# A two-layer block on one core: how the slots' weights are turned, where W_out is loaded, and who normalises the last two groups

## The chip, the cores and the metric

The kernel runs on one core of one Trainium2 chip, as a single program. Its time is device microseconds of one execution, from the first instruction to the last with what lies around them; three executions are timed, and their median is the figure. One further execution is recorded by the hardware profiler and gives the profile.

The core has five engines that run in parallel, each through its own instructions in a fixed order: TensorE (PE, matrix products and 128 x 128 transposes against an identity), VectorE (DVE), ScalarE (ACT), GpSimd (POOL) and SyncE (SP, which here only issues DMAs). PEld is PE's loading of the stationary operand.

## The reference

The input x has 32 sequences of 512 tokens with 256 features, all in float32. Two layers are added to it, each after a layer norm without weights:

```python
x = x + attn(_layernorm(x), ...)
x = x + ffn(_layernorm(x), ...)

def attn(x):      # causal, one head
    q = tanh(x @ W_charge.T + b_charge)[..., 0]
    phi_c = mags * q[..., None] ** arange(5)
    shell = x @ W_shell.T + b_shell;  shell = shell / norm(shell)
    proj = shell @ omega.T + rff_bias
    phi = outer(phi_c, concat[cos(proj), sin(proj)]) @ W_combine.T
    attn = softmax(causal(phi @ phi.T * T / temp))
    return (attn @ (x @ W_v.T + b_v)) @ W_out.T + b_out

def ffn(x):       # 64 slots, each token takes its best 8
    h = gelu(concat[x, slot_mean] @ w1.T + b1)
    alpha = softmax over the top 8 of (h @ w2.T + b2) / (|tau| + 0.1), else 0
    gi = einsum('bts,btd->bsd', alpha, x) / (alpha.sum(1) + 1e-8)
    h_new = GRU(gi, slots)
    slot_values = h_new @ wv.T + bv
    return einsum('bts,bsd->btd', alpha, slot_values) @ wo.T + bo
```

`alpha` is needed with tokens on the partitions for the sum into the slots, and with slots on the partitions (turned) for the product that gives the slots' values back to the tokens.

## The kernel before

**Tiles and groups.** Two sequences make a group; there are 16 groups. A tile is 128 tokens x 256 features, so a group has 8 tiles. Each group goes through `features` (stages tokens, angles, phi), `attention` (weights, values), `router` (normal, router) and `slots` (taken, gru, given). The main tiles are named after their group: `xT` (x turned), `pf` and `sv` (the product of x with the folded weights `wf`, in PSUM and in SBUF), `phi`, `pl`, `pr`, `po` (logits, weights and output of attention; tile group 3 is the last row of 128 tokens, `pl_0` covers tokens 0 and 1), `xm` (the normalised x of the second layer), `xmT` (it, turned), `ph` (hidden layer), `prr`, `prt`, `rl` (router logits), `al` (alpha, L1510), `psi` (sum into the slots, L1534), `gi`, `prz`, `pn`, `rz`, `nn`, `rh`, `hn` (GRU), `alT` (alpha turned, L1655 and L1662), `pv`, `val` (slots' values) and `py` (what is given back, L1692; DVE adds it to x at L1706 and SP stores it).

**Who turns what.** PE turns a 128 x 128 block through PSUM (name `pt...`), and another engine copies it out. For x (from group 2 on) and xm (but in the last two groups, `LAST_BY_TENSOR = 2`) another way is used: a DMA writes the tile to memory (`xd`), four DMAs read it back so that each 32 x 32 block lies where it will have to be (`xmb`, `xb`), and DVE's transpose, which works block by block, does the rest (`xT`, L929; `xmT`, L881).

**The order.** Nothing runs in the order of the source. Each step is added to a plan with its engine, a cost, the steps that it follows and the buffers that it uses (`add`). `Plan.order` then places the steps one at a time: on each engine the ready step that could start first, ties by rank. A rank is made of the step's earliest time in its group (weighted with `LATE` against its latest), the group's number times `STRIDE`, and two numbers of its stage in `DELAY`, the second for the last groups. `HOP` is the plan's cost of going from one engine to another, `SWITCH` a penalty for changing PE's shape. So a change of these numbers changes the order of every engine's instructions, SP's DMAs included, and each engine then goes through its list in order and waits where an operand is missing. In the program each DMA issued by SP or ACT also waits for the landing of the eighth one before it.

**The start.** SP loads W_v, x_0 and x_1, small weights, x_2, the rest of the weights; ACT's queue loads W_charge, W_shell, W_out and two biases. DVE centres W_v (L432 to L435), PE multiplies it with W_out (`pw`, L446) into `wf`, which the first `pf` needs. The last setup steps on PE are `pt_hs` and `pgh` (L763, of the GRU's weights whh).

Of the kernel before, what the change touches and what calls it, by code (L numbers as in the profile page):

```python
# [23 lines left out]
SQ = 32  # L24
BY_TENSOR = 2
LAST_BY_TENSOR = 2
# [31 lines left out]
    "xT": 3,  # L58
    "xmT": 2,
    "xd": 2,  # L60
    "sv": 2,
    "xm": 2,
    "al": 2,
# [8 lines left out]
}  # L72


HOP = 0.23
TABLE = 1.28
SWITCH = 2.05
STRIDE = 33.83
LATE = 0.0

DELAY = {
    "setup": (0.0, 0.0),
    "load": (-30.3, -13.9),
    "tokens": (2.1, -9.2),
    "angles": (-45.8, -2.6),
    "phi": (5.7, -20.1),
    "weights": (-1.3, -2.7),
    "values": (18.9, -12.8),
    "normal": (16.1, 19.2),
    "router": (1.5, -3.5),  # L90
    "taken": (-8.0, -7.1),
    "gru": (26.3, -22.0),
    "given": (43.2, -16.5),
}

SPARE = 3
# [22 lines left out]
class Plan:  # L119
# [126 lines left out]
def block_kernel(ctx: ExitStack, tc: tile.TileContext, a: dict, out: bass.AP):  # L246
    nc = tc.nc
    x = a["x"]
    B = x.shape[0]
    NG = B // GB  # L250
# [7 lines left out]
    def lazy(tag, name, shape, dtype=F32):  # L258

        if tag not in pools:  # L260
            space = {"ps": bass.MemoryType.PSUM, "xd": bass.MemoryType.DRAM}.get(tag)
# [78 lines left out]
    ident = const("ident", [P, P])  # L340
# [20 lines left out]
    hs = const("hs", [P, D])  # L361
# [51 lines left out]
    def value_and_out(wv_ap, bv_ap, wo_t_ap, bo_ap, w_dst, b_dst, n, centred, engs, rank):  # L413

        at = 2 * n
        wv = part(at, 0, [P, KD, D])
        wo_t = part(at, KD * D, [P, KD, D])
        bv_rep = part(at, 2 * KD * D, [P, KD, P])
        bo = part(at, 2 * KD * D + KD * P, [P, D])
        of = wv.of  # L420
        bv = const(f"bv{n}", [P, KD])
        mean = const(f"wv_mean{n}", [P, KD])
        land = 3.5 if centred else None
        l_wv = load(engs[0], wv, rows(wv_ap), 256, rank=rank, land=land)
        l_wo = load(engs[1], wo_t, rows(wo_t_ap), 256, rank=rank, land=land)
        l_bv = load(engs[2], bv, bv_ap.rearrange("(k p) -> p k", p=P), 8, rank=rank)
        l_bo = load(engs[2], bo, bo_ap.partition_broadcast(P), 128, rank=rank)
        last = l_wv
        if centred:

            def centre():
                nc.vector.tensor_reduce(mean, wv(), AX.X, ALU.add)  # L432
                nc.vector.tensor_scalar(mean, mean, 1.0 / D, None, ALU.mult)
                for k in range(KD):
                    nc.vector.tensor_scalar(  # L435
                        wv()[:, k, :], wv()[:, k, :], mean[:, k : k + 1], None, ALU.subtract
                    )

            last = add("DVE", 1.6, centre, [l_wv], of, rank=rank)
        done, made = [], []  # L440
        for m in range(KD):
            pw = bank(f"pw{n}_{m}")

            def project(m=m, pw=pw):
                for k in range(KD):
                    nc.tensor.matmul(  # L446
                        pw()[:, 0:D],
                        wv()[:, k, m * P : (m + 1) * P],
                        wo_t()[:, k, :],
                        start=(k == 0),  # L450
                        stop=(k == KD - 1),
                    )
# [13 lines left out]

        def spread():
            for k in range(KD):
                nc.vector.tensor_scalar(
                    bv_rep()[:, k, :], onesP, bv[:, k : k + 1], None, ALU.mult  # L470
                )

        s = add("DVE", 0.5, spread, [l_bv, s_ones], of, rank=rank)
        pb = bank(f"pb{n}")

        def project_bias():
            for k in range(KD):
# [19 lines left out]
        return done, made  # L497
# [7 lines left out]
        bias_f[:, C_V:NF],  # L505
        0,
        True,
        ("SP", "ACT", "POOL"),
        -40.0,
    )  # L510
    l_bsh = [
# [15 lines left out]
    s = add("PE", 0.8, mean_shell, l_sh + [s_ones] + s_wv_pe, [pm], rank=-38.0)  # L527
# [5 lines left out]
    for q in range(P // SQ):  # L533
        for k in range(KD):
# [9 lines left out]
                    land=4.0,  # L544
# [7 lines left out]
    for bb in range(GB):  # L552
        r = slice(bb * SHELL, (bb + 1) * SHELL)
        for h in range(2):
# [15 lines left out]
                land=5.0,  # L570
# [146 lines left out]
    s = add("PE", 0.3, hs_transposed, [s_hs, s_ident], [pt_hs], rank=41.0)  # L717
# [16 lines left out]
    s = add("PE", 0.8, mean_hidden, [s_hst, l_w1s], [pb1] + w1s.of, rank=42.0)  # L734
# [612 lines left out]
    def router(g, s_x, ln):  # L1347

        xt = xs[g]
# [33 lines left out]
        def deviations():  # L1383
# [3 lines left out]
            nc.gpsimd.tensor_tensor(nmr, nm, rs, ALU.mult)  # L1387

        s_ln = add("POOL", 2.25, deviations, s_sq, [ln])
        s_xm = [  # L1390
            add(
                "ACT",
                0.51,
                lambda t=t: nc.scalar.activation(  # L1394
                    xm()[:, t, 0:D],
                    xt()[:, t, :],
                    AF.Identity,
                    bias=ln()[:, 4, t // NT, t % NT : t % NT + 1],
                    scale=ln()[:, 1, t // NT, t % NT : t % NT + 1],
                ),  # L1400
                [s_ln, s_one],
                [xm, xt, ln],
            )
# [96 lines left out]
        def sums():  # L1500
# [4 lines left out]
        s = add("DVE", 1.53, sums, [s], [rl, rest, asum])  # L1505
        s_al = [
            add(
                "POOL",
                1.1,
                lambda: nc.gpsimd.tensor_tensor(  # L1510
                    al().rearrange("p c b s -> p (c b) s"),
                    rl(),
                    asum().unsqueeze(2).to_broadcast([P, GT, SLOTS]),
# [8 lines left out]
    def slots(g, xm, al, s_al):  # L1522
# [48 lines left out]

        gi_t, s = halves("gi", gi, s_gi)
        plan.stage = "gru"

        rz = lazy("row", f"rz_{g}", [P, 2 * D])
        nn = lazy("half", f"nn_{g}", [P, D])
# [5 lines left out]
        def gates(dst, lo, n):  # L1582
# [42 lines left out]
            [rz, rh],  # L1625
        )
        s = add(
            "POOL",
            0.73,
            lambda: nc.gpsimd.tensor_tensor(nn(), nn(), rh(), ALU.add),  # L1630
            [s, s_n],
            [nn, rh],
        )
        s_nn = add("ACT", 0.42, lambda: nc.scalar.activation(nn(), nn(), AF.Tanh), [s], [nn], "exp")
        s = add(
            "POOL",
            0.73,
            lambda: nc.gpsimd.tensor_tensor(rh(), hs, nn(), ALU.subtract),
            [s_nn],
            [rh, nn],  # L1640
        )
# [5 lines left out]
        s = add("DVE", 0.94, new_state, [s], [rz, rh, nn, hn])  # L1647

        plan.stage = "given"
        pta = bank(f"pta_{g}")  # L1650
        al_t = lazy("row", f"alT_{g}", [P, T])

        def weights_turned():
            for c in range(NT):
                nc.tensor.transpose(  # L1655
                    pta()[:, c * P : (c + 1) * P],
                    al()[:, c, :, :].rearrange("p b s -> p (b s)"),
                    ident,
                )

        s_pta = add("PE", 0.58, weights_turned, s_al, [al, pta, al_t])
        s_alt = add("ACT", 0.54, lambda: nc.scalar.copy(al_t(), pta()), [s_pta], [pta, al_t])  # L1662

# [133 lines left out]
```

## Time and profile before

| | |
|---|---|
| timed runs | 699.04, 699.42, 700.35 us; median 699.42 |
| profiled execution | 698.51 us, its span 696.7 |
| PE busy | 665.6 us (96%) |
| DVE busy | 569.4 us (82%) |
| ACT busy | 461.5 us (66%) |
| POOL busy | 208.6 us (30%) |
| 128 x 128 transposes of `al` on PE (L1655) | 64, 273 ns each |
| copies of them out on ACT (L1662) | 16, 566 ns each |
| DMA | 83.26 MB, mean 120 GB/s |

The span runs from the first instruction to the last. A busy time is the union of an engine's instructions. Matmuls overlap, so that four transposes of 273 ns take less than their sum: the distance from one step's start to the next one's start is what PE really spends. A float32 matmul of the source appears as two records. In a line of the waits, the first name waits and the one after the arrow ended the wait; then total, times and the longest.

### The profile page before, as it was taken

The page shows a single profiled execution, that of the slowest core. Times are in us where ns is not written, and L with a number is a line of the kernel's source. Part 1 is how long each engine was busy: PE and PEld are TensorE (multiplying, and loading weights), DVE is VectorE, ACT ScalarE, POOL GpSimd, SP SyncE. Part 2 cuts the span into 40 slices and gives each one's busy share as a digit, 9 for nine tenths or more (in the row PEclk, how much of TensorE's full clock was granted, in tenths as well). Part 3 has the DMA queues.
Part 4 walks back from the last instruction along what each step waited for, and adds up shares of the span by engine and source line. Part 5 has one row for each costly group of instructions (what it writes and reads, how often), then busy time and mean ns, then how long its engine had stood idle before and what let it go on. Part 6 is the DMA issues. An engine that isn't in the chain of part 4 may idle for free.

```text
span 696.7 us, 12314 instructions
## 1 busy us (share of the span) xinstructions
PE 665.6 (96%) x3946; PEld 457.3 (66%) x3946; DVE 569.4 (82%) x1790; ACT 461.5 (66%) x1081; POOL 208.6 (30%) x406
## 2 busy tenths in 40 slices
PE   3979999999999999999999999999999999999975
PEld 3747766767666676766676676767667666667533
DVE  3979779789796988989798898979798896966554
ACT  1437777767766676775867677677677667778840
POOL 3640333124252232313333132323322224211120
PEclk9989999999999999999999999999999999999999
DMA  6683351552633735363544446263542611400203
GB/s 179 166 232 97 126 117 62 122 181 62 190 97 78 217 86 182 83 199 82 149 125 122 152 110 194 62 179 94 152 149 63 213 30 56 127 1 32 90 1 121
DMA packets 174256, 83.26 MB, mean 120 GB/s; under 512 B 123664, under 2 KB 173392, under 8 KB 174192
## 3 DMA queue, kind: packets, MB, share of 16 engines
q1 hardware_dynamic: 172880, 81.95, 42.2%
q8 instruction: 31, 0.51, 0.3%
q10 hardware_dynamic: 1104, 0.36, 0.2%
q14 instruction: 33, 0.27, 0.1%
q0 software_dynamic: 208, 0.17, 0.1%
HBM read 50.67 MB, written 31.46 MB: 118 GB/s over the span
## 4 chain that ended last, share of the span: by engine, by line
PE 83%; DVE 5%; ACT 4%; DMA 3%; SPq 2%; issue 1%; POOL 1%; DVEq 0%; POOLq 0%; ACTq 0%
PE po L1305 20%; PE pf L959 16%; PE ph L1422 8%; PE ptp L1299 5%; PE pl L1221 5%; PE pph L1164 5%; PE psi L1534 4%; PE py L1692 4%; PE prz L1584 3%; DMA x<-in_x_dram 2%; SPq L280 2%; PE prr L1445 2%; PE pv L1672 2%; PE pn L1584 2%; PE pp L1106 1%; ACT xm L1394 1%
## 5 line engine op out<-in xcount | busy, mean ns | idle before, releaser
L1305 PE MATMUL po<-sv,prT 128*128 128x256 f32 x640 | 150.5, 379 | 0.0
L959 PE MATMUL pf<-wfb,xT 128*128 128x321 f32 x448 | 129.0, 438 | 0.0
L1305 PEld LDWEIGHTS po<-sv,prT 128*128 128x128 f32 x640 | 116.5, 189 | 16.7 <-issue 1.1
L959 PEld LDWEIGHTS pf<-wfb,xT 128*128 128x128 f32 x448 | 82.3, 189 | 37.4 <-issue 3.9
L1262 ACT ACTIVATE pr<-lg,nm 128x128 f32<-128x128 f32 (+3 forms) x128 | 70.3, 550 | 15.4 <-DVE nm L1250 15.0
L1334 DVE SCALAR_TENSOR_TENSOR x<-po,den,x 128x256 f32<-128x256 f32 x128 | 58.0, 478 | 24.3 <-PE po L1305 23.1
L1394 ACT ACTIVATE xm<-x,lnb 128x256 f32<-128x256 f32 x128 | 66.3, 590 | 10.1 <-POOL lnb L1387 10.1
L1371 ACT ACTIVATE xm<-x,lnb 128x256 f32<-128x256 f32 x128 | 63.6, 501 | 5.9 <-POOL lnb L1359 5.8
L972 DVE SCALAR_TENSOR_TENSOR sv<-pf,lna,bias_f 128x321 f32<-128x321 f32 x128 | 62.7, 540 | 3.2 <-PE pf L959 2.6
L1510 POOL TENSOR_TENSOR al<-rl,asum 128x512 f32<-128x512 f32 x16 | 16.7, 1043 | 143.6 <-DVE asum L1503 142.0
L1250 DVE CUSTOM_DVE_ANT_0 lg<-pl,mask 128x128 f32<-128x128 f32 (+3 forms) x128 | 55.8, 480 | 3.2 <-PE pl L1221 2.8
L1317 ACT COPY prT<-ptp 128x384 f32<-128x384 f32 (+1 forms) x96 | 46.6, 511 | 13.8 <-PE ptp L1299 13.5
L1422 PE MATMUL ph<-xmT,w1b 128*128 128x512 f32 x112 | 52.5, 596 | 0.0
L1706 DVE TENSOR_TENSOR x<-py,x 128x512 f32<-128x512 f32 x64 | 40.0, 683 | 14.0 <-PE py L1692 14.0
L1359 POOL TENSOR_SCALAR lnb<-lnb 128x2 f32<-128x2 f32 (+1 forms) x48 | 12.1, 253 | 128.3 <-DVE x L1334 128.1
L1299 PE MATMUL ptp<-ident,pr 128*128 128x128 f32 x320 | 48.3, 276 | 1.0 <-ACT pr L1262 0.9
L800 DVE BATCH_NORM_STATS2 bna<-x 128x6 f32<-128x256 f32 x128 | 47.1, 414 | 0.0
L1299 PEld LDWEIGHTS ptp<-ident,pr 128*128 128x128 f32 x320 | 37.3, 140 | 13.7 <-issue 6.3
L1221 PE MATMUL pl<-phi 64*128 64x256 f32 (+1 forms) x384 | 45.3, 361 | 0.0
L1221 PEld LDWEIGHTS pl<-phi 64*128 64x128 f32 x384 | 31.2, 186 | 15.5 <-issue 7.6
L1152 DVE TENSOR_TENSOR tp<-tp,qs 128x1024 f32<-128x1024 f32 x32 | 39.2, 1225 | 2.2 <-ACT tp L1138 1.7
L1164 PE MATMUL pph<-tp,wc 64*64 64x256 f32 x640 | 38.2, 381 | 0.0
(169 smaller groups left out, 1252.5 us busy)
## 6 DMA issues: line engine op xcount, KB each, us to landing
x<-in_x_dram SPq DMA_DIRECT2D x32, 512.0 KB, 5.0
out_dram<-x SPq DMA_DIRECT2D x64, 256.0 KB, 2.5
xb<-in_x_dram SPq DMA_DIRECT2D x112, 128.0 KB, 2.7
xd<-xm SPq DMA_DIRECT2D x28, 512.0 KB, 4.4
xmb<-xd SPq DMA_DIRECT2D x112, 128.0 KB, 2.7
setup<-in_gru_whh_t_dram SPq DMA_DIRECT2D x1, 768.0 KB, 6.5
wih<-in_gru_wih_t_dram SPq DMA_DIRECT2D x1, 768.0 KB, 9.8
wfb<-wf SPq DMA_DIRECT2D x8, 40.1 KB, 3.4
```

The lines of the kernel that those rows point to most:

```text
L959: nc.tensor.matmul(pf()[:, 0:NF], tile_()[:, k, c * P : (c + 1) * P], w[:, k, :], start=(k == 0), stop=(k == KD - 1),)
L972: lambda t=t, pf=pf: nc.vector.scalar_tensor_tensor(sv()[:, t, :], pf()[:, 0:NF], ln()[:, 1, t : t + 1], bias_f, ALU.mult, ALU.add,),
L1164: nc.tensor.matmul(phs[h]()[bb * COMB : (bb + 1) * COMB, 0:HT], wc[r, m, :], tp()[r, m, bb * HT : (bb + 1) * HT], start=(m == 0), stop=(m ...
L1221: nc.tensor.matmul(pls[bb]()[:, off[i] + lo : off[i] + lo + w], phi()[r, 0, q : q + P], phi()[r, 1, k : k + w], start=True, stop=True,)
L1250: nc.vector.tensor_tensor_reduce(out=lg()[:, c], in0=pls[bb]()[:, c], in1=mask[:, T - w : T], scale=1.0, scalar=TOP, op0=ALU.add, op1=ALU.min,
L1262: nc.scalar.activation(pr()[:, c], lg()[:, c], AF.Exp, bias=nm(), scale=-1.0, accum_out=den()[:, tiles.index(i), bb : bb + 1],)
L1299: nc.tensor.transpose(pt()[:, j : j + P], prs[bb]()[:, j : j + P], ident)
L1305: nc.tensor.matmul(po()[:, d * D : (d + 1) * D], pr_t()[:, lo : lo + P], sv()[:, bb * NT + j, C_V:NF], start=(j == 0), stop=(j == i),)
L1334: nc.vector.scalar_tensor_tensor(xt()[:, t, :], po()[:, d * D : (d + 1) * D], den()[:, d, bb : bb + 1], xt()[:, t, :], ALU.mult, ALU.add, ...
L1371: lambda bb=bb, i=i: nc.scalar.activation(xm()[:, bb * NT + i, 0:D], xt()[:, bb * NT + i, :], AF.Square, bias=ln()[:, 2, bb, i : i + 1], a ...
L1394: lambda t=t: nc.scalar.activation(xm()[:, t, 0:D], xt()[:, t, :], AF.Identity, bias=ln()[:, 4, t // NT, t % NT : t % NT + 1], scale=ln()[ ...
L1422: nc.tensor.matmul(ph(), w1[:, k, :], dst()[:, k, :], start=(k == 0), stop=(k == KD - 1))
```

## The change

It does five things.

1. *The slots' weights.* In groups 0 to 13 `al` is written to memory by one DMA (`ad`, 256 KB), read back by four (`ab`, 64 KB each, in runs of 32 floats) and turned block by block by one DVE transpose into `alT`. The four PE transposes and ACT's copy stay in groups 14 and 15 only.
2. *W_out* is issued by SP after W_v and before the tokens, and no longer by ACT.
3. *xm of the last two groups* is made by DVE with a multiply and an add per token tile, in place of ACT's Identity with scale and bias.
4. *POOL's steps of the last two groups*: `al`, and two sums of the GRU (`nn`, `rh`), go to DVE.
5. *Ranks.* `HOP`, `SWITCH`, `STRIDE`, `LATE` and all of `DELAY` have new values, so that every engine's order is a new one. In a middle group the attention's tile groups now go 3, 2, 0 in place of 0, 2, 3, and the slots' `py` of group g stands among the logits of group g + 3.

```diff
-HOP = 0.23
+HOP = 0.44
 TABLE = 1.28
-SWITCH = 2.05
-STRIDE = 33.83
-LATE = 0.0
+SWITCH = 0.0
+STRIDE = 21.62
+LATE = 0.74

 DELAY = {
...
-    "load": (-30.3, -13.9),
-    "tokens": (2.1, -9.2),
...
-    "given": (43.2, -16.5),
+    "load": (-12.3, 2.7),
+    "tokens": (6.7, -6.0),
...
+    "given": (4.5, 5.6),
 }
...
-    ("SP", "ACT", "POOL"),
+    ("SP", "SP", "POOL"),
...
+        by_vector = g >= NG - LAST_BY_TENSOR
+
+        def moved(t):
+            b, c = divmod(t, NT)
+            bias, scale = ln()[:, 4, b, c : c + 1], ln()[:, 1, b, c : c + 1]
+            if by_vector:
+                nc.vector.tensor_scalar(
+                    xm()[:, t, 0:D], xt()[:, t, :], scale, bias, ALU.mult, ALU.add
+                )
+            else:
+                nc.scalar.activation(
+                    xm()[:, t, 0:D], xt()[:, t, :], AF.Identity, bias=bias, scale=scale
+                )
...
-                "POOL",
-                1.1,
-                lambda: nc.gpsimd.tensor_tensor(
+                "DVE" if by_vector else "POOL",
+                0.7 if by_vector else 1.1,
+                lambda: (nc.vector if by_vector else nc.gpsimd).tensor_tensor(
                     al().rearrange("p c b s -> p (c b) s"),
...
+        by_vector = g >= NG - LAST_BY_TENSOR
+        side, cost = ("DVE", 0.42) if by_vector else ("POOL", 0.73)
+        ev = nc.vector if by_vector else nc.gpsimd
...
-            lambda: nc.gpsimd.tensor_tensor(nn(), nn(), rh(), ALU.add),
+            lambda: ev.tensor_tensor(nn(), nn(), rh(), ALU.add),
...
-            lambda: nc.gpsimd.tensor_tensor(rh(), hs, nn(), ALU.subtract),
+            lambda: ev.tensor_tensor(rh(), hs, nn(), ALU.subtract),
...
+        if g >= NG - LAST_BY_TENSOR:
...
+        else:
+            ad = lazy("ad", f"ad_{g}", [T, P])
+            ab = lazy("row", f"ab_{g}", [P, T // SQ, SQ])
+            s_a = add("SP", 0.7,
+                lambda: nc.sync.dma_start(
+                    out=ad().rearrange("(c p) s -> p c s", p=P),
+                    in_=al().rearrange("p c b s -> p c (b s)"),
+                ), s_al, [al, ad], land=3.3)
+            s_b = []
+            for q in range(P // SQ):
+                def back(q=q):
+                    nc.sync.dma_start(
+                        out=ab()[q * SQ : (q + 1) * SQ, :, :],
+                        in_=ad().rearrange("(t i) (q e) -> q i t e", i=SQ, q=P // SQ)[q],
+                    )
+                s_b.append(add("SP", 0.6, back, [s_a], [ad, ab], land=3.8))
+            s_alt = add("DVE", 0.63,
+                lambda: nc.vector.transpose(al_t(), ab().rearrange("p t e -> p (t e)")),
+                s_b, [ab, al_t])
```

Line numbers of the kernel before are those of its profile; the changed kernel's are higher by 1 from the first edit on and by more after each further one.

More of the change, by code (lines that the diff above doesn't have):

```diff
@@ L60 @@
     "xd": 2,
+    "ad": 2,
     "sv": 2,
@@ L72 @@
 }
-HOP = 0.23
+HOP = 0.44
 TABLE = 1.28
-SWITCH = 2.05
-STRIDE = 33.83
-LATE = 0.0
+SWITCH = 0.0
+STRIDE = 21.62
+LATE = 0.74
 DELAY = {
     "setup": (0.0, 0.0),
-    "load": (-30.3, -13.9),
-    "tokens": (2.1, -9.2),
[L85 to L92, printed above, removed]
-    "given": (43.2, -16.5),
+    "load": (-12.3, 2.7),
+    "tokens": (6.7, -6.0),
+    "angles": (-34.4, -22.3),
+    "phi": (-0.8, -14.6),
+    "weights": (0.1, -9.6),
+    "values": (6.3, -2.2),
+    "normal": (5.3, -2.9),
+    "router": (0.2, 8.3),
+    "taken": (-2.2, -3.4),
+    "gru": (11.7, -3.8),
+    "given": (4.5, 5.6),
 }
@@ L260, in lazy @@
         if tag not in pools:
-            space = {"ps": bass.MemoryType.PSUM, "xd": bass.MemoryType.DRAM}.get(tag)
+            space = {"ps": bass.MemoryType.PSUM, "xd": bass.MemoryType.DRAM, "ad": bass.MemoryType.DRAM}.get(tag)
             kind = {"space": space} if space else {}
@@ L422, in value_and_out @@
         mean = const(f"wv_mean{n}", [P, KD])
-        land = 3.5 if centred else None
+        land = 3.3 if centred else None
         l_wv = load(engs[0], wv, rows(wv_ap), 256, rank=rank, land=land)
@@ L1389, in router @@
         s_ln = add("POOL", 2.25, deviations, s_sq, [ln])
+        by_vector = g >= NG - LAST_BY_TENSOR
[10 more added lines that the diff above has]
+                )
         s_xm = [
             add(
[L1392 to L1400, printed above, removed]
+                "DVE" if by_vector else "ACT",
+                0.25 if by_vector else 0.51,
+                lambda t=t: moved(t),
                 [s_ln, s_one],
@@ L1627, in slots @@
         s = add(
-            "POOL",
-            0.73,
-            lambda: nc.gpsimd.tensor_tensor(nn(), nn(), rh(), ALU.add),
+            side,
+            cost,
+            lambda: ev.tensor_tensor(nn(), nn(), rh(), ALU.add),
             [s, s_n],
@@ L1635, in slots @@
         s = add(
-            "POOL",
-            0.73,
-            lambda: nc.gpsimd.tensor_tensor(rh(), hs, nn(), ALU.subtract),
+            side,
+            cost,
+            lambda: ev.tensor_tensor(rh(), hs, nn(), ALU.subtract),
             [s_nn],
@@ L1649, in slots, with weights_turned @@
         plan.stage = "given"
-        pta = bank(f"pta_{g}")
         al_t = lazy("row", f"alT_{g}", [P, T])
[L1653 to L1662, printed above, removed]
+        if g >= NG - LAST_BY_TENSOR:
+            pta = bank(f"pta_{g}")
+            def weights_turned():
+                for c in range(NT):
+                    nc.tensor.transpose(
+                        pta()[:, c * P : (c + 1) * P],
+                        al()[:, c, :, :].rearrange("p b s -> p (b s)"),
+                        ident,
+                    )
+            s_a = add("PE", 0.58, weights_turned, s_al, [al, pta, al_t])
+            s_alt = add("ACT", 0.54, lambda: nc.scalar.copy(al_t(), pta()), [s_a], [pta, al_t])
+        else:
+            ad = lazy("ad", f"ad_{g}", [T, P])
+            ab = lazy("row", f"ab_{g}", [P, T // SQ, SQ])
+            s_a = add(
+                "SP",
+                0.7,
+                lambda: nc.sync.dma_start(
+                    out=ad().rearrange("(c p) s -> p c s", p=P),
+                    in_=al().rearrange("p c b s -> p c (b s)"),
+                ),
+                s_al,
+                [al, ad],
+                land=3.3,
+            )
+            s_b = []
[4 more added lines that the diff above has]
+                        in_=ad().rearrange("(t i) (q e) -> q i t e", i=SQ, q=P // SQ)[q],
+                    )
+                s_b.append(add("SP", 0.6, back, [s_a], [ad, ab], land=3.8))
+            s_alt = add(
+                "DVE",
+                0.63,
+                lambda: nc.vector.transpose(al_t(), ab().rearrange("p t e -> p (t e)")),
+                s_b,
+                [ab, al_t],
+            )
         hn_t, s = halves("hn", hn, s)
```

## The prediction

> **What bounds the kernel.** I read the page first, then the windows over two steady groups, the waits of the TensorE (PE), its timeline in one group, the DMAs of the first 60 us, and the chain at the end.
>
> ```profile
> span 696.7 us, 12314 instructions
> PE 665.6 (96%) x3946; PEld 457.3 (66%) x3946; DVE 569.4 (82%) x1790; ACT 461.5 (66%) x1081; POOL 208.6 (30%) x406
> PE   3979999999999999999999999999999999999975
> ```
>
> ```profile
> core 0: us, PE busy (x) PEld busy (x) DVE busy (x) ACT busy (x) POOL busy (x), PEclk, DMA share, GB/s
> 381.80:421.70 39.90, 39.90 (x246) 27.42 (x244) 35.03 (x112) 28.03 (x66) 12.17 (x25) 1.00 0.48 133
> 421.70:461.60 39.90, 39.90 (x246) 27.42 (x244) 35.04 (x112) 28.03 (x66) 12.16 (x25) 1.00 0.48 133
> ```
>
> Between its ramps the kernel repeats one group in 39.90 us, and PE has no idle time in it: a microsecond of PE work removed there is a microsecond won, as long as nothing else takes 39.9 us. VectorE (DVE) is next with 35.03.
>
> ```profile
> PE pw L446 <- DMA setup<-in_W_out_t_dram: 10.5, 1, 10.5
> PE pt_hs L715 <- DVE hs L708: 3.7, 1, 3.7
> PE psi L1534 <- POOL al L1510: 2.4, 2, 1.6
> PE prt L1451 <- ACT rlT L1459: 1.5, 1, 1.5
> ```
>
> PE's waits are the first product's 10.5 us for W_out, a few more in the first 45 us, and the end.
>
> ```profile
> 399.74 0.60 PE L1655 MATMUL pta<-ident,al 128*128 128x128 f32 x4
> 400.18 1.88 PE L1584 MATMUL prz<-wih,giT 128*128 128x512 f32 x4
> ```
>
> Start to start, the four transposes of one group's weights hold PE for 0.44 us.
>
> ```profile
> setup<-in_W_v_dram SPq DMA_DIRECT2D x1, 256.0 KB, 3.7
> setup<-in_W_out_t_dram ACTq DMA_DIRECT2D x1, 256.0 KB, 8.5
> ```
>
> W_v is first on SP's queue and lands 3.7 us after its issue; W_out, of the same size, is third on ACT's, beside 2 MB of tokens, and takes 8.5.
>
> ```profile
> 653.63 1.97 ACT xm L1394 x4
> ...
> 665.41 1.05 POOL al L1510
> ...
> 674.13 1.05 POOL al L1510
> ```
>
> At the end the chain leaves PE and goes through ACT's normalisation and POOL's steps, the ones that the change moves.
>
> **Part 1, the weights' turn in 14 of 16 groups.** Per group it removes four PE transposes (0.44 us) and an ACT copy (0.56 us, ACT is busy for 28.0 of 39.9: worth nothing by itself). It adds one DMA out (256 KB), four back (64 KB each) on SP and one DVE transpose (the row of the same shape, xmT, has 0.68 us). 14 x 0.44 = **-6.1 us**, if the group stays bound by PE. Three covers:
> - *Latency.* The nearest DMAs are xd (512 KB, 4.4 us to land) and xmb (128 KB, 2.7, longest 4.2). Out 4.4, four issues of 0.5, back 2.7 and 0.7 on DVE make 9.8 us. In the new order the weights are used by `py` a round and more after `psi` of the same group, over 40 us later. Covered even if SP holds it back for 20 us.
> - *SP.* Its issues go from 24 to 29 a group, at about 0.48 us 11.5 to 13.9 us of 39.5. SP works in order, so what stands behind the new ones matters: `xmb` of the next group (for xmT, hence `ph`) stands partly behind the stores, which wait for the last `x` adds of `py`. I place the last xmb at 4 us of the round, landed at 6.6, wanted by DVE at 9.6. Covered by 3 us.
> - *DVE.* 35.03 + 0.68 = 35.7 of 39.46 us. It waits in order too; it may idle for 3.8 us a group before it sets the pace, and idles for 4.87 now. This is the cover that can fail.
>
> [...] I go by the rows, since they show one engine without idle time and one with 4.87 us.
>
> The pieces going back are 128 bytes long. [...]
>
> **Part 2, W_out on SP ahead of the tokens.** In place of 10.46 us the first product can start when W_v is centred: DVE's two L435 steps end at 6.35 us. That is at most -4.1. The gain then meets things that don't move. Each DMA in the program waits for the landing of the eighth before it; so SP issues x_2 after x_1's second half has landed (tau's issue, 15.18 us), as before, and then all weights one by one. whh, issued at 35.18, lands 6.5 us later at 41.7. `pgh` needs it and began at 44.33. So at most -2.6 arrives there; `hs`, which PE waited 3.7 us for, now stands ahead of `rn_1` on DVE and no longer binds. After it, group 0's attention has little beside it, and the new ACT order loads two tables (1.28 us each) ahead of group 0's first `pr`; by placing each step at its row's time I get PE at the end of group 2's `pf` 2.9 us ahead for the same work. Bounds 0 (tokens that land later eat it) and -4.1; I take **-2.7**, by the whh row.
>
> **Part 3, new ranks.** I laid the new order of one round against PE's pitches. The nearest margins: `py` waits for `val`, on DVE behind all eight `sv` and `rn` (0.3 us to spare); `psi` for `al`, POOL's 1.04 us after DVE's `asum` (0.5); `pt_hn` for `hn` (0.5); `pl_3` for `phi` (1.3). All else has over 1 us. The placing isn't that exact. Bounds: nothing, as in the order of before, and 0.7 us a group over 12 groups (Rival 1's size), +8.2. Nearest is the row without idle time; I allow 0.1 us a group, **+1.2 us**. Behind a wait of `py` stand group 11's last transposes and `po`, behind one of `psi` the GRU of that group, all on PE.
>
> **Part 4, the last two groups.** Removed: ACT's 16 `xm` (0.59 us each), POOL's two `al` (1.04) and four `nn`/`rh` (0.73). Added on DVE: 16 tensor_scalars (the L708 row, 128x256, has 0.34), two 128x512 products (0.69), four of 128x256 (0.42). Before, group 15's `xm` ran from 651.48 to 656.56 on ACT; on DVE it is 8 x 0.34 = 2.7 us, so `ph_15` may end some 2.4 us earlier. But the new PE order puts `py_13` (1.93 us) ahead of `prt_15`, and `val_13` waits on DVE behind eight `top_14` (3.7 us); `al_14`, then `rz_14` and `nn_14`, stand ahead of `al_15` there too. By my placing `al_15` ends about 1 us later after prt_13 than the 52.8 us of before; POOL's two steps on the last GRU give back 2 x 0.31 and a handover. Net **0**. Bounds: -5 (xm 2.4, al 2 x 0.35, nn and rh 1.2, and 0.7 where `py` doesn't bind) and +3 (py_13 and the queue of DVE).
>
> **Sum.** -6.1 - 2.7 + 1.2 + 0 = -7.6 us. The profiled execution took 698.51 us (span 696.7, 1.8 around it): 690.9. The median of the three timed runs, 699.42, lies 0.91 above the profiled one, so I predict **691.8 us**.
>
> **Rivals.**
> 1. *VectorE sets the pace* (the other side). If it keeps its 4.87 us of idle time a group, because it still waits for the same PE, ACT and POOL results in order, a round is 35.71 + 4.87 = 40.6 us in place of 39.9: +0.7 over 12 rounds, +8.2, less 2.7 of the start: 698.51 + 5.5 + 0.91 = 704.9. It decides from 0.73 us of PE waits a group on: 12 x 0.73 eats the 6.1 and the 2.7. For it: 91% of DVE's time is taken, in one fixed order. Against: 4.2 of the 4.87 us are waits for PE (`phi` 1.7, `py` 1.2 ...), which shrink when DVE is late.
> 2. *The start is hidden anyway*: tokens, not W_out, set it. Then -6.1 + 1.2: 694.5. For it: x_1's landing at 15.1 paces SP. Against: PE is busy from 10.46 to 37.9 without a wait.
> 3. *The end gains its bound*: -12.6: 686.8. For it: every step named is on the chain of before. Against: DVE's queue.
> 4. *The change doesn't do what it says*: the PE time removed comes back as waits of 0.65 us a group: 698.51 - 8.8 + 7.8 + 0.91 = 698.4. For it: margins of 0.3 and 0.5 us. Against: no group of before shows one.
>
> **How the numbers follow.** My forecast has 0.45 (own range 689 to 694.5), rival 2 0.18, rival 3 0.14, rival 4 0.10, rival 1 0.13. A measurement of this kernel can tell some 0.2%, 1.4 us: 698.0 to 700.8 counts as the same. Faster takes the forecast, rivals 2 and 3 and a little of 4: 0.79; same 0.05 from 4; slower 0.16 from 1 and the rest of 4. The range, 685.5 to 700.0, reaches from below rival 3 to the upper end of 4, and leaves out rival 1 and the tails.
>
> **What would show it.** Right: steady rounds of 39.4 to 39.6 us with PE idle under 0.2, DVE 35.7, no pta before group 14, `pw` starting near 6.4 us, `pgh` near 42, the last 53 us (after group 15's last `po`) within 3 of that. Wrong: rounds of 40 us or more with PE waiting for `val`, `al`, `hn` or `phi` (Rival 1 or 4); `pw` early but `pgh` at 44 (Rival 2); the stretch after the last `po` at 48 (Rival 3). The forecast fails most easily on DVE's order, which I placed by hand.

## The result and the profile after

The changed kernel is slower: 701.43 us, the median of 13 runs (699.63 to 702.62), against 699.04 us for 13 runs of the kernel before beside them (697.23 to 700.72). The ratio is 1.003, with a 95% interval of 1.002 to 1.004. Its profiled execution took 701.82 us with a span of 700.0 us, 3.3 us more than the span of 696.7 before. I had said 691.8 us, and 0.79 for faster.

The page of the changed kernel, its first lines and PE in 40 slices:

```profile
span 700.0 us, 12341 instructions
...
PE 663.6 (95%) x3890; PEld 455.7 (65%) x3890; DVE 593.1 (85%) x1826; ACT 444.4 (63%) x1051; POOL 204.0 (29%) x400
...
PE   6969999999999999999999999999999999999865
```

PE has 56 instructions less, as foreseen, but its busy time is only 2.0 us less, and it is idle for longer. Two rounds in the middle, by windows from one `pph` to the next (length, then the busy time of each engine):

```profile
core 0: us, PE busy (x) PEld busy (x) DVE busy (x) ACT busy (x) POOL busy (x), PEclk, DMA share, GB/s
377.88:418.35 40.47, 39.71 (x239) 27.23 (x237) 36.38 (x112) 27.22 (x65) 12.73 (x25) 1.00 0.56 144
418.35:458.87 40.52, 39.70 (x239) 27.21 (x237) 36.42 (x112) 27.22 (x65) 12.60 (x25) 1.00 0.54 144
```

A round takes 40.5 us in place of 39.90, and PE is idle for 0.8 us of it. DVE has 36.4 us of work where I had said 35.7. The waits of PE (us in total, times, longest) say where:

```profile
PE pt_hn L1568 <- DVE hn L1658: 7.4, 10, 1.3
PE pw L447 <- DVE setup L436: 6.0, 1, 6.0
PE psi L1544 <- DVE al L1520: 5.3, 2, 3.4
PE pt_hs L716 <- DVE hs L709: 4.4, 1, 4.4
...
PE pl L1222 <- DVE phi L1180: 0.9, 1, 0.9
```

The transposes of the new state, `pt_hn`, wait in every steady round. The timeline in front of one such wait (start, duration, in brackets the idle time of the engine ahead of it and what ended that):

```profile
425.90 0.74 DVE L1495 TENSOR_TENSOR rl<-rl,top 128x512 f32<-128x512 f32 x1
...
426.71 1.28 ACT L1504 ACT_TABLE_LOAD   x1 [4.40 <-DVE rl L1495]
...
428.01 0.72 ACT L1504 ACTIVATE rl<-rl,rtau 128x512 f32<-128x512 f32 x1
...
428.76 0.69 DVE L1511 SCALAR_TENSOR_TENSOR rl<-rest,rl 128x512 f32<-128x512 f32 x1 [0.44 <-ACT rl L1504]
...
430.49 1.11 POOL L1520 TENSOR_TENSOR al<-rl,asum 128x512 f32<-128x512 f32 x1 [3.27 <-DVE asum L1513]
...
430.74 1.15 DVE L1658 SCALAR_TENSOR_TENSOR hn<-rh,nn 128x256 f32<-128x256 f32 x1
...
431.94 0.44 PE L1568 MATMUL pt_hn<-ident,hn 128*128 128x128 f32 x2 [0.70 <-DVE hn L1658]
```

Two things are to be seen. ScalarE stood idle for 4.40 us and then loaded the table of exp only when DVE's `rl` was there, so that 1.28 us lie between two steps of DVE; DVE stood for 0.44 us of them. And `hn`, which takes 0.43 us when it runs alone, took 1.15: it began 0.25 us after POOL's `al` and ended 0.28 us after it. PE loses more than the 0.70 us: from the start of the last `pf` to the start of the first `psi` it takes 1.69 us, against 0.60 in experiment 3, where nothing waits. The last `pf` has nothing to overlap with (1.13 us to the first `pt_hn` in place of 0.27), and from there to `psi` it is 0.56 us in place of 0.33.

At the start the first product does begin early. W_out lands 4.3 us after its issue (8.5 before), `pw` begins at 6.02 us and `pgh` at 41.34 (44.33 before). Then this follows:

```profile
49.66 0.71 DVE L930 STREAM_TRANSPOSE xT<-xb 128x512 f32<-128x512 f32 x1 [3.10 <-DMA xb<-in_x_dram]
50.30 0.39 DVE L1180 TENSOR_TENSOR phi<-pph,dec_q 128x256 f32<-128x256 f32 x1
...
51.40 2.83 PE L1222 MATMUL pl<-phi 64*128 64x256 f32 x24 [0.94 <-DVE phi L1180]
```

DVE waits 3.10 us for group 3's tokens ahead of group 0's `phi`, and PE waits 0.94 us for `phi`. At the end VectorE's `xm` and `al` run as costed:

```profile
650.95 3.29 DVE L1398 TENSOR_SCALAR xm<-x,lnb 128x256 f32<-128x256 f32 x8
...
667.00 0.69 DVE L1520 TENSOR_TENSOR al<-rl,asum 128x512 f32<-128x512 f32 x1
...
676.74 0.68 DVE L1520 TENSOR_TENSOR al<-rl,asum 128x512 f32<-128x512 f32 x1
```

but the stretch behind the last `po` is 55.2 us where it was 53.0.

### The profile page after: what moved, and what is told of

Same layout as the page of the kernel before. It is cut to its first block, busy times and chain, and to the rows that moved or that the text cites. A ratio compares the mean times of both kernels' runs of the same rounds, so it can differ in the third digit from the quotient of the medians.

```text
span 700.0 us, 12341 instructions
## 1 busy us (share of the span) xinstructions
PE 663.6 (95%) x3890; PEld 455.7 (65%) x3890; DVE 593.1 (85%) x1826; ACT 444.4 (63%) x1051; POOL 204.0 (29%) x400
## 4 chain that ended last, share of the span: by engine, by line
PE 72%; DVE 15%; DMA 5%; ACT 3%; SPq 2%; issue 1%; DVEq 0%; ACTq 0%
PE po L1306 20%; PE ph L1432 7%; PE pf L960 7%; PE ptp L1300 5%; PE pph L1165 5%; PE psi L1544 5%; PE pl L1222 4%; PE py L1739 4%; PE prz L1597 4%; DVE rest L1487 3%; DMA x<-in_x_dram 2%; PE prr L1455 2%; PE pv L1719 2%; SPq L281 2%; DVE phi L1180 2%; PE pn L1597 2%
## 5 line engine op out<-in xcount | busy, mean ns | idle before, releaser
L1263 ACT ACTIVATE pr<-lg,nm 128x512 f32<-128x512 f32 (+3 forms) x128 | 70.4, 551 | 4.8 <-DVE nm L1251 4.6
L1372 ACT ACTIVATE xm<-x,lnb 128x256 f32<-128x256 f32 x128 | 63.5, 501 | 1.9 <-POOL lnb L1360 1.8
L1251 DVE CUSTOM_DVE_ANT_0 lg<-pl,mask 128x512 f32<-128x512 f32 (+3 forms) x128 | 56.4, 482 | 4.1 <-PE pl L1222 2.8
L1402 ACT ACTIVATE xm<-x,lnb 128x256 f32<-128x256 f32 x112 | 56.8, 587 | 4.3 <-POOL lnb L1388 4.3
L1300 PE MATMUL ptp<-ident,pr 128*128 128x128 f32 x320 | 49.7, 278 | 0.1
L801 DVE BATCH_NORM_STATS2 bna<-x 128x6 f32<-128x256 f32 x128 | 45.1, 411 | 1.6 <-DMA x<-in_x_dram 1.6
L1300 PEld LDWEIGHTS ptp<-ident,pr 128*128 128x128 f32 x320 | 36.7, 140 | 14.4 <-issue 9.4
L930 DVE STREAM_TRANSPOSE xT<-xb 128x512 f32<-128x512 f32 x56 | 38.5, 696 | 3.1 <-DMA xb<-in_x_dram 3.1
```

Source lines behind the costliest of these rows:

```text
L1251: nc.vector.tensor_tensor_reduce(out=lg()[:, c], in0=pls[bb]()[:, c], in1=mask[:, T - w : T], scale=1.0, scalar=TOP, op0=ALU.add, op1=ALU.min,
L1263: nc.scalar.activation(pr()[:, c], lg()[:, c], AF.Exp, bias=nm(), scale=-1.0, accum_out=den()[:, tiles.index(i), bb : bb + 1],)
L1300: nc.tensor.transpose(pt()[:, j : j + P], prs[bb]()[:, j : j + P], ident)
L1372: lambda bb=bb, i=i: nc.scalar.activation(xm()[:, bb * NT + i, 0:D], xt()[:, bb * NT + i, :], AF.Square, bias=ln()[:, 2, bb, i : i + 1], a ...
L1402: nc.scalar.activation(xm()[:, t, 0:D], xt()[:, t, :], AF.Identity, bias=bias, scale=scale)
```

## The experiments

**Theory.** The round is longer because the new state comes late: the new order puts `rh` and `hn` on DVE right behind the three sums, hence behind the table load, and beside `al`. **Rival.** DVE, with 36 us of ordered work in a round, has become the bound (my first rival): a wait taken away at one place comes back at another. "Rounds" below are from one `pph` to the next in the middle of each profile. Medians are each compared with runs of the kernel before on the same chip; the ratios have 95% intervals.

**1. The table ahead of its use.** ScalarE gets one more, tiny, activation:

```diff
+        def candidate():
+            nc.scalar.activation(nn(), nn(), AF.Tanh)
+            if 2 <= g <= 10:
+                nc.scalar.activation(warm, nhalf[:, 0:1], AF.Exp)
...
```

> The changed kernel, with one small Exp on ScalarE behind the candidate's Tanh of groups 2 to 10, so that the table of exp is loaded while ScalarE is idle and not behind VectorE's rl; every other instruction and order is kept. Theory (late state: in each steady round PE waits 0.68 us for hn, and loses another 0.34 us in starting again, because hn stands on VectorE behind a chain with a table load of 1.28 us, and because POOL's al slows hn itself from 0.43 to 1.15 us): VectorE waits 0.44 us for the exp now, so hn comes about 0.5 us earlier and the wait falls from 0.68 to about 0.2; rounds go from 40.50 to about 40.0 us, 9 rounds, 4.5 us in all: 697. Rival (VectorE's load: VectorE has 36 us of work a round in a fixed order, and a wait that is taken away at one place comes back at another): rounds stay at 40.5, the time within 1 us of 701.4.

Rounds of 39.93 us, 0.56 less. The wait for `hn` fell from 0.70 to 0.11 us, although `hn` itself still took 1.15. The median is 699.64 us (ratio 1.0017, 1.0005 to 1.0029), above the 697 expected: in its profile the first `pl` waited 3.1 us for `phi` in place of 0.9. That wait at the start lies between 0.9 and 3.1 us in the seven profiles whose first 60 us have the same order. So the round speaks for the theory, while the total carries the start too.

**2. The state ahead of the sums.** Two entries of VectorE's list change places, for eight groups:

```diff
...
+        if names == ["sums", "new_state"] and steps[sv].cost == 0.42:
+            steps[sv], steps[state] = steps[state], steps[sv]
```

> The changed kernel, with the new state of eight groups (rh and hn, 0.8 us) and one sv of VectorE in each other's place: the state now stands ahead of the sums and not behind them. Nothing else moves. Theory (late state): hn is ready some 2.5 us before PE wants it and no longer runs beside POOL's al, so it takes 0.43 us in place of 1.15; the wait of pt_hn is gone, al comes when it came and psi may wait 0.1 to 0.2 us for it; rounds of 39.6 to 39.7 us in place of 40.5, eight of them, 6 to 7 us in all: 694 to 695.5. Rival (VectorE's load): the wait goes to psi, to py or to the next phi, rounds stay above 40.3, 700 to 701.5.

694.04 us (ratio 0.9938, 0.9924 to 0.9952), as the theory said. The windows of two rounds:

```profile
334.54:374.10 39.56, 39.48 (x238) 27.10 (x236) 35.72 (x112) 27.11 (x65) 12.65 (x25) 1.00 0.56 147
374.10:413.67 39.57, 39.49 (x238) 27.10 (x237) 35.73 (x112) 27.11 (x65) 12.67 (x25) 1.00 0.56 147
```

DVE's load falls by 0.7 us with the same instructions, since `hn` takes 0.43 us again. Only `psi` now waits, for 0.08 us a round, and no other wait took the place of the one removed. The first rival falls: with all of its work in one order DVE lets PE go on in rounds of 39.57 us.

**3. Both edits.**

> The changed kernel with both edits, the early table and the state ahead of the sums. Theory (late state): rounds of 39.46 to 39.55 us, as 39.90 less the 0.44 of the four transposes, PE without a wait in a steady round; 8 to 9 us less than the changed kernel, 692 to 693.5. Rival (VectorE's load): no more than 1 us below the better of the two edits alone, rounds above 40.

```profile
335.98:375.41 39.43, 39.43 (x238) 27.09 (x237) 35.59 (x112) 27.54 (x66) 12.66 (x25) 1.00 0.67 148
375.41:414.86 39.45, 39.45 (x239) 27.12 (x237) 35.60 (x112) 27.55 (x66) 12.68 (x25) 1.00 0.66 147
```

PE is busy for the whole round, 39.44 us. That is the round that I had forecast. In time it is 694.31 us (ratio 0.995, 0.9934 to 0.9967), no better than the second edit alone: the first `pl` waited 2.3 us in its profile (1.1 in that of experiment 2).

**4. POOL's `al` in four pieces**, at the place of the one:

```diff
...
+                    (nc.vector if by_vector else nc.gpsimd).tensor_tensor(
+                        al().rearrange("p c b s -> p (c b) s")[:, n : n + GT // 4, :],
...
+                    for n in range(0, GT, GT // 4)
```

> The changed kernel with al's product made in four pieces of 128x128 in place of one of 128x512, at the same place of the same engine. Theory (VectorE's hn waits for the end of whatever POOL instruction runs beside it): hn takes 0.43 us and what is left of one piece, at most 0.3, so 0.5 to 0.75 us in place of 1.15, and the wait of pt_hn falls to 0.2 to 0.4 us; al ends a little later and psi may wait. Rival (both are slowed by sharing, as long as they run together): hn stays at 1.0 to 1.15 us, since the four pieces follow each other without a break.

(In the last two groups VectorE's `al` is cut in the same way.) Two rows of its timeline:

```profile
426.83 1.72 POOL L1521 TENSOR_TENSOR al<-rl,asum 128x128 f32<-128x128 f32 x4 [3.11 <-DVE asum L1513]
427.08 0.50 DVE L1661 SCALAR_TENSOR_TENSOR hn<-rh,nn 128x256 f32<-128x256 f32 x1
```

`hn` takes 0.50 us though POOL works beside it the whole time, and the steady wait of `pt_hn` is gone. Rounds are 39.83 us, 0.67 less. One run of 693.85 us, to which a shorter end also adds (53.0 us behind the last `po`). So `hn` was not slowed by sharing, but held until the POOL instruction that it began beside had ended: it ends 0.28 us behind that one's end both times, behind the whole `al` of 1.11 us and here behind the first piece of 0.47. POOL's second piece was held in turn (0.58 us, the third and fourth 0.39).

By its rows PE has no idle time ahead of `pt_hn` in this run, and still the round is 0.39 us longer than that of experiment 3: 0.43 us from the last `pf` to `pt_hn` in place of 0.27, and 0.55 from there to `psi` in place of 0.33. In this run a result that came only just in time cost PE overlap on both sides, 0.16 us and 0.22 us.

**5. The turn alone, in the order of before.** The DMA out stands behind `al`, the four back at `pv`'s place, the turn on VectorE behind `val`; PE's transposes and ScalarE's copy are left out of 14 groups.

> The kernel before, in its own order on every engine, with the weights' turn by way of memory and VectorE alone (14 groups): the four transposes and the copy are left out, the DMA out stands behind al, the four back behind pv's place in the order, the turn on VectorE behind val. Theory (the turn itself is worth what PE loses by it): rounds of 39.46 us in place of 39.90, 14 x 0.44 = 6.1 us less than the kernel before: 693. Rival (VectorE's load): the 0.68 us more on VectorE delays what stands behind it, and PE waits for xmT or for x; rounds of 39.9 to 40.6, 699 to 705.

697.86 us, a ratio of 1.0001 (0.9986 to 1.0016): nothing won. Rounds are 39.76 us, 0.15 less and not 0.44. The timeline, which is that of the longest of the twelve executions (701.34 us), shows what the transposes had covered:

```profile
440.41 0.44 PE L1559 MATMUL pt_gi<-ident,gi 128*128 128x128 f32 x2
...
440.89 0.37 ACT L1567 COPY giT<-pt_gi 128x256 f32<-128x256 f32 x1 [1.05 <-PE pt_gi L1559]
441.31 0.30 PEld L1585 LDWEIGHTS prz<-wih,giT 128*128 128x128 f32 x2 [0.26 <-ACT giT L1567]
```

In the old order `ptq` and the weights' transposes lie between `pt_gi` and `prz`; without the latter `prz` waits for ScalarE's copy. Besides, `py` waits for the turned weights four times (1.5 us in all), and the first `pph` came 0.9 us later in this profile.

**6. The transposes back on PE** in the kernel with both edits, first right behind `psi`:

> The kernel with the early table and the state ahead of the sums, with the weights of the first 14 groups turned by PE's four transposes again, right behind psi, and copied by ScalarE; the DMAs and VectorE's turn are left out. Theory (with no wait in its rounds PE pays the transposes in full): rounds of 39.88 us in place of 39.44, 14 x 0.44 = 6.1 us more, 700 to 701. Rival (as in the old order, where the transposes covered the latency of giT and only 0.14 us a round were won): rounds of 39.5 to 39.6, 696.

711.37 us (ratio 1.018, 1.016 to 1.02), rounds of 41.05: neither theory had this. ScalarE's copy of the weights stood ahead of its copy of the state, and `pv` waited 0.95 us a round for the latter. So this run prices the place and not the transposes. Then, in the kernel of experiment 10, at the place where VectorE's turn stands:

> The kernel with the mended start, with the weights of the first 14 groups turned by PE's four transposes and copied by ScalarE, now at the place in the order where VectorE's turn stands, behind pn and ahead of prr; the DMAs and VectorE's turn are left out. Theory (in a round without waits PE pays the transposes in full): rounds of 39.85 to 39.9 us in place of 39.44, no new wait, 14 x 0.44 = 6.1 us more than 690.8: 696 to 697.5. Rival (here too the transposes cover something, the h_t that prr waits for): rounds of 39.5 to 39.6, 692 to 693.

PE's steps `pn` and `pta` take 1.39 us from start to start in place of 0.96 for `pn` alone: the 0.44 us are paid in full, nothing is covered. Besides, `psi` waits 0.26 us for `al` in seven rounds, so that these take 40.19 us. It is the hold of experiment 4 at another place: POOL's `rh` comes 1 us earlier in the round than in experiment 10, and VectorE's step ahead of exp begins beside it and takes 1.00 us in place of 0.69:

```profile
423.77 0.73 POOL L1690 TENSOR_TENSOR rh<-hs,nn 128x256 f32<-128x256 f32 x1
...
424.05 1.00 DVE L1528 TENSOR_TENSOR rl<-rl,top 128x512 f32<-128x512 f32 x1
```

In the last groups `prr` waits 1.3 and 2.7 us for `h_t`. In all 705.85 us (ratio 1.0103, 1.0081 to 1.0126), more than the 697 expected: the span is 14.4 us longer than in experiment 10, of which 6.1 are the transposes and 5.7 more idle time of PE, while 2.6 stay without an account.

**7. W_out alone, in the order of before.** One DMA moves from ScalarE's queue to SP's, right behind W_v.

> The kernel before, with W_out alone issued on SP right behind W_v; nothing else moves. Theory (the first product's early start arrives in part): pw starts at 6.0 to 6.4 us in place of 10.46, pgh at 41.4 to 42 in place of 44.3; behind it VectorE's turn of a later group's tokens stands ahead of phi and waits for those tokens, so that 1 to 1.5 of the 2.9 us are lost again: 1.4 to 1.9 us less than the kernel before, 696.4 to 697. Rival 2 of the prediction (hidden anyway): within 0.7 us of the kernel before. If all of it arrived: 2.7 less.

695.1 us (ratio 0.9955, 0.9937 to 0.9974), a span of 693.7 in place of 696.7. `pw` starts at 6.03 us, `phi` and `pl` wait for nothing but PE, and the steady rounds are as before. More than I had expected here, and about what the prediction had. Of the 3.2 us that `pgh` is earlier (41.15 us), 2.3 are still there when the last group's first `pph` starts (611.1 us in place of 613.5); the other 0.6 of the span lie behind the last `po`, where nothing was changed, and where profiles of one order differ by as much (those of the new order's end have 54.2 to 56.1 us there).

**8. The last two groups on the old engines, in the new order.**

> The changed kernel with the last two groups' normalisation on ScalarE again and their al, nn and rh steps on POOL, each issued at the place in the order where VectorE's step stands now. Theory (VectorE's queue at the end: al of the last two groups, 3.4 and 1.9 us of waits of psi in place of 1.6 and 0.8, is late because VectorE has got more to do there): the stretch behind the last po goes from 55.2 us to between 53 and 54, 1 to 2 us less than the changed kernel, 699.4 to 700.4. Rival (the order is what costs, not the engine): the same stretch or up to 3 us more, as eight xm at 0.59 us in place of 0.34 are 2 us later: 701 to 704.5.

706.05 us (ratio 1.0104, 1.0088 to 1.012), 0.74% or 5 us above the changed kernel, where I had expected 1 to 2 us less. By the spans it is 4.1 us: the stretch behind the last `po` is 57.7 us (55.2), and 1.1 us of the rest are the first `pl`. In this order VectorE is the right engine for these steps.

**The same steps on VectorE in the order of before:**

> The kernel before, in its own order, with the last two groups' normalisation, al, nn and rh on VectorE alone. Theory (in the new order the same change is worth 3 to 4.6 us; here VectorE has less in its queue at the end): the stretch behind the last po falls from 53.0 us to 48 to 50, 3 to 5 us less than the kernel before: 693.5 to 695.5. Rival (VectorE's queue eats it): within 1 us of the kernel before.

699.4 us, a ratio of 1.0015 (1.0004 to 1.0025): no gain, slightly a loss. The stretch is 53.4 us in place of 53.0; `al` of the last group waits in VectorE's queue (`psi` 1.8 us in place of 0.8).

**9. The ranks alone, and all but the ranks.** Both change numbers only, and the order is made anew.

> The kernel before with the new values of the ranks alone, from which the order of every engine is made anew (it is not quite the changed kernel's order: the transposes are PE's again, and the state stands ahead of the sums on VectorE). Theory (a round costs what PE has to do, and more only where a result is late; the state ahead of the sums is in time): rounds of 39.9 to 40.2 us, 698 to 702. Rival (the new ranks are the worse order whatever stands where): rounds of 40.5 us and more, 704 and more.

> The changed kernel with the values of the ranks as before, from which the order is made anew: the turn by memory, W_out on SP and the last two groups on VectorE, all but the new ranks. Theory (the ranks decide only where results are late): no steady wait for hn, the transposes are gone from PE, but the order was not made for these steps and single waits appear: rounds of 39.5 to 40.5 us, 690 to 702. Rival (an order made anew is mostly worse, as the new ranks alone were with 718.6): above 705.

718.57 us (ratio 1.0293, 1.0272 to 1.0315) and 728.32 us (1.0425, 1.0398 to 1.0453). Neither has a steady round: the first goes 37.6, 41.1, 41.0, 38.2, 43.9 us, the second repeats 49.6, 37.8 and 38.1, and ends with waits of 6.6 and 10.0 us for `hn` and `al`. My range was wrong for both. Ranks and steps belong together, and the cost of the ranks by themselves can't be had by exchanging them.

**10. The start.** With both edits, first VectorE's turn of group 3's tokens alone moved behind `phi`:

> The kernel with the early table and the state ahead of the sums, and besides two of VectorE's steps at 50 us moved: the turn of group 3's tokens now stands behind group 0's phi and group 1's nearest, and not ahead of them. Theory (VectorE waits there for the landing of group 3's tokens, 3.1 to 4.6 us in the runs so far, and holds back phi, for which PE waits 0.9 to 3.1 us): the wait of the first pl is under 0.3 us, what was lost of the early start comes back in part, 1 to 2 us less than without this edit: 692.3 to 693.3. Rival (something else takes as long: tables on ScalarE, the tokens themselves): PE waits as long at ptp or po, same time as without it, 694.3.

The wait moved instead of going:

```profile
PE pw L469 <- DMA setup<-in_wo_t_dram: 4.0, 1, 4.0
```

The new order issues wo on SP behind group 3's tokens, and its product on PE stands ahead of group 0's transposes. 697.2 us (ratio 0.9981, 0.9965 to 0.9998). So both are moved:

```diff
...
+    rest = rest[:n] + weights + rest[n:]     # wv, wo ahead of group 3's tokens on SP
+    n = rest.index(last) + 1                 # the turn of these behind group 0's last lowest
+    return rest[:n] + late + rest[n:]
```

> The kernel with the early table and the state ahead of the sums, and the start in another order: the loads of wv and wo are issued on SP ahead of group 3's tokens, and VectorE's turn of those tokens (and SP's loads of group 4's behind it) stand behind group 0's last lowest. Theory (in the changed kernel's start two things stand in the way of the gain: VectorE waits for group 3's tokens ahead of phi, and where that wait was moved away PE waited 4.0 us for wo): neither pl nor the second pw waits more than 0.3 us, the early start arrives as it does in the old order (3.0 us), rounds stay at 39.44: 690 to 691.5. Rival (something else takes as long): a third wait of 1 us and more between 48 and 62 us, time as without it, 694.

690.81 us (690.52 to 691.15), a ratio of 0.9887 (0.9872 to 0.9902): 7.9 us faster than the kernel before and faster than both. Its rounds, and the first `pl`:

```profile
332.13:371.57 39.44, 39.44 (x238) 27.10 (x236) 35.60 (x112) 27.54 (x66) 12.67 (x25) 1.00 0.69 147
371.57:411.02 39.45, 39.45 (x239) 27.11 (x237) 35.60 (x112) 27.54 (x66) 12.69 (x25) 1.00 0.66 147
```

```profile
49.99 2.60 PE L1255 MATMUL pl<-phi 64*128 64x256 f32 x24
```

## Why the prediction was wrong

| Term of the sum | predicted | measured | by |
|---|---|---|---|
| the turn off PE, 14 groups | -6.1 | -6.5 | 14 x (39.906 - 39.439), the steady rounds of before and of experiment 3, neither with a wait |
| W_out ahead of the tokens | -2.7 | -2.3 to -3.0 in the old order, about -1.4 in the new | experiment 7; `pgh` 3.0 us earlier, less the waits of `pl` and `po` behind it, 0.9 and 0.7 us |
| new ranks | +1.2 | about +8.9 | 8 x (40.49 - 39.44), and a ninth wait of 0.5 us |
| the last two groups | 0 | +2.2 | 55.2 - 53.0 behind the last `po` |
| sum | -7.6 | +3.2; the spans +3.3 | see below |

The first and third terms are good to some tenths. The start and the end are not: kernels with the same order at the end have 54.2 to 56.1 us behind the last `po`, so that the close sum is in part luck.

**The step that failed is Part 3**, the margin of "0.5" for "`pt_hn` for `hn`", and with it the 0.1 us a group that I allowed for all margins. Measured, this one costs 1.05 us a round: 0.70 us of waiting, and 0.35 in the steps on both sides of the wait. The placing had let exp follow `rl` at once and had given `hn` its 0.43 us. Both were wrong: a load of 1.28 us stands ahead of exp, 0.44 us of which VectorE stood idle, and `hn` took 0.72 us more. Taking away either leaves `pt_hn` a wait of 0.11 us or none and wins most of the 1.05 us, though not all: the first 0.56 us a round (experiment 1), the second 0.67 (experiment 4). The first stood in the trace of before: there the same load (11 times 1.28 us, in front of the exp at L1494) also came only after DVE's `rl`, where nothing urgent stood behind it. The plan names exp's table at the candidate's Tanh already, so that its `TABLE` cost falls ahead of the wait; in the trace of the changed kernel no table is loaded between the Gelu of `h_t` and that Tanh in 11 of 16 groups (the Tanh at 421.90 us takes 0.42 us with no load ahead of it), and the load of 1.28 us comes only in front of the exp. The second could not be read off `hn` in the trace of before, since in the old order it never ran beside `al`. But that trace holds three other VectorE instructions that began beside one of POOL and took 0.23 to 0.42 us longer than their like, of which this is one (0.69 us elsewhere):

```profile
567.77 0.84 POOL L1630 TENSOR_TENSOR nn<-nn,rh 128x256 f32<-128x256 f32 x1 [5.77 <-DVE nn L1612]
568.06 1.10 DVE L1131 SCALAR_TENSOR_TENSOR turn<-turn,ang 128x512 f32<-128x512 f32 x1
```

Two of these three and the `rl` of experiment 6 have 128x512 elements and end 0.55 us behind POOL's; the third has 128x256, as `hn` does, and ends 0.28 us behind. `sv`, which reads one operand from PSUM, was not held: it began beside `al` 14 times in the trace of before and took at most 0.04 us more than its shortest.

**Part 1** was right in its mechanism and size in the new order, by experiment 6 too, and its three covers held: neither SP nor the landings (2.9 us out, 2.8 back, in the pieces of 128 bytes) show in a steady round. What I left out is that it depends on the order: in the old one only 0.15 us a round were to be had (experiment 5), as the transposes covered the latency of `giT`. VectorE's idle time, by which I went, had the room: in experiment 3 its 0.7 us for the turn cost nothing, with PE busy for the whole round of 39.44 us.

**Part 2** was right for `pw` (6.02 us). For `pgh` (41.34, said 41.7) the number came out by luck: whh, issued at 35.66 us, landed 4.6 us later at 40.30, and not at 41.7, so it was not what `pgh` waited for. Nor did `hs` cease to bind: `pt_hs` waited 4.4 us for it, and `pgh` followed behind that step and `pb`. Behind `pgh` it was wrong. I followed PE and the weights and missed that VectorE's queue now had the tokens of group 3 ahead of `phi`, and SP's queue these tokens ahead of wo. Rival 2 ("tokens, not W_out, set it") was so half right, at 50 us and not at 15.

**Part 4**: `xm` came as worked out (the last `ph` 2.3 us earlier after the last `po`) and so did the delay of the last `al` ("about 1 us later", measured 1.1). Net 0 was the middle of wide bounds, and +2.2 lies inside them. What I had not split is that the order at the end and the engine pull in opposite ways: on the old engines the new order's end is 4.7 us longer than before (57.7 against 53.0), and VectorE gives 2.5 of them back.

Of the rivals, number 4 (waits that eat PE's time, 0.65 us a group, 698.4) named the mechanism and a wait within 0.05 us of the one measured, but not that PE loses half as much again in starting. Rival 1 had nearly the right round (40.6 us) for the wrong reason, as experiment 2 shows. The first of the signs of a wrong forecast that I listed is the one that came: rounds above 40 us with PE waiting for `hn`.

Not settled is why the wait for group 3's tokens differs so much between profiles of the same order (0.9 to 3.1 us at `pl`), nor why the end differs by up to 2 us.

## What to carry to other kernels

When an order is replaced as a whole, place the new one with everything that can stand between two steps, table loads (1.28 us each here) and POOL's work beside VectorE's (0.72 us more for `hn`) included, and treat a margin of half a microsecond as a wait until a row shows otherwise: here one of 0.5 us became a wait of 0.70. What is removed from the busiest engine is won only where what it covered was not needed (of 0.44 us a round 0.15 were won in the old order, all of it in the new one): look at what the next instruction waits for without it. And when a change has several parts, look for the one late result before judging the parts: here two entries exchanged in one engine's list turned +0.3% into -0.6%, and with the table and the start mended it was -1.1%.

## What the runs showed that I had not expected

- `hn`, which reads SBUF alone, was held when it began beside POOL's `al` (1.15 us in place of 0.43, its end 0.28 us behind POOL's all eight times), `sv`, which reads PSUM, was not (at most 0.04 us), and cutting `al` into four made the hold short (`hn` 0.50 us) at the price of POOL's own time (1.72 us in place of 1.04).
- The wait of PE cost more than its length: 0.70 us of idle time cost 1.05 us of the round, and in experiment 4 no idle time at all cost 0.39 us.
- An activation of 128x1, whose result nobody reads, was worth 0.56 us a round, by when it made the table load (0.13 us with the state ahead of the sums, by the rounds of experiments 2 and 3).
- The same eleven steps of each of the last two groups, on VectorE in place of ScalarE and POOL, were worth about 3 us in one order by the spans (4.1, of which 1.1 lie at the start), and nothing in the other.
